# Graph attention over 32 graphs: softmax weights made as [source, target] without turns, scores and sums as extra columns, rows spread through HBM, stages of three graphs interleaved

## The chip, the core and the metric

The kernel runs on one NeuronCore of a Trainium2 chip. The metric is device time in microseconds (us) from the first to the last instruction of one launch. The inputs lie in HBM, 32 graphs of 512 nodes with 512 features each, and everything is computed in float32 except the masks.

## The reference

Each graph goes through a layer norm and a ReLU, then through two graph-attention layers, and the input is added at the end. Cut to what is computed:

```
def gat_layer(x, mask, W, a_src, a_dst, bias, concat):      # H heads of F features
    xl = (x @ W).reshape(B, N, H, F)
    asrc = einsum('bnhf,hf->bnh', xl, a_src)                 # score of a node as source
    adst = einsum('bnhf,hf->bnh', xl, a_dst)                 # score of a node as target
    e = leaky_relu(asrc[:, :, None, :] + adst[:, None, :, :], 0.2)
    e = where(mask[..., None], e, -1e9)
    attn = softmax(e, axis=1)                                # over the sources
    out = einsum('bsdh,bshf->bdhf', attn, xl)
    return (out joined over heads, or their mean) + bias

mask = (adj > 0) | eye
h = relu(layernorm(x))
h = elu(gat_layer(h, mask, W1, as1, ad1, b1, concat=True))   # 4 heads of 256
y = x + gat_layer(h, mask, W2, as2, ad2, b2, concat=False)   # 1 head of 512
```

## The kernel before

All tiles have 128 partitions, and a graph's 512 nodes make four blocks of 128. A framework schedules the program: the code gives the operations and the pools of buffers, and the framework decides the order of each engine's queue and sets the semaphores. So the code's order is only a start, and what stands behind what on an engine has to be read from the built program. Each engine works through its queue in order. All DMAs are issued by SyncE (SP).

The main loop runs over the graphs, b = 0 to 31. `front(b)` normalises x (VectorE), turns it on TensorE to [feature, node] (`pht`, line 139, through an identity matrix), and turns the mask to [target, source] in bf16 (`pm`, line 153). GpSimd adds the second bias to x (line 141).

First layer. `scores` multiplies the four 128-row pieces of the turned input with a narrow matrix `v1` of 8 columns (W applied to the attention vectors; `prow`, line 162), turns the rows back to columns (`pcol`, line 167), and `softmax` spreads one row of scores over all 128 partitions by a product with a selecting matrix of 8 or 2 rows (`bc`, line 178). For each block of targets and each head it then computes the scores on ScalarE (line 185), the leaky ReLU on VectorE (line 186), mask and minimum in one instruction (line 187), and the exponential with its sum on ScalarE (line 191). The product x @ W1 (`pxl`, line 223) has 512 columns to a matmul and is copied out of PSUM by ScalarE (line 227). For each head, VectorE divides the weights by their sums (line 233), `turned` turns them to [source, target] with sixteen transposes on TensorE (`ppt`, line 204) and four copies on VectorE (line 205), and the aggregation (`po`, line 240) gives [feature, target]. Bias and ELU follow on VectorE and ScalarE (lines 247 to 251).

Second layer. The same with one head: narrow scores `prow` with 2 columns, `bc`, softmax, the product with W2 (`pxm`, line 264, copied at line 269), four `ppt` groups, the aggregation (`po`, line 276), then scale, add and store (line 280).

PSUM has eight banks: three for the products (`mm`), two for turns (`tp`), two for the spread rows (`bc`), one for scores. A float32 matmul appears in the profile as two instructions, each with a weight load of its own on PEld; a float32 transpose as one.

Of the kernel before, what the change touches and what calls it, by code (L numbers as in the profile page):

```python
# [8 lines left out]
F32 = mybir.dt.float32  # L9
# [4 lines left out]
PSUM = bass.MemoryType.PSUM  # L14

P = 128
# [12 lines left out]
def tile_gat(  # L29
# [30 lines left out]
    assert N == 512 and D == 512 and DO == D and HF % 512 == 0  # L60
# [3 lines left out]
    psum = ctx.enter_context(tc.tile_pool(name="psum", bufs=1, space=PSUM))  # L64

    X, ADJ = {}, {}

    def load(b):
        X[b] = work.tile([P, NT, D], F32, tag="x", name=f"x{b}")
        nc.sync.dma_start(X[b], x[b].rearrange("(t p) d -> p t d", p=P))  # L70
        for t in range(NT):
            a = work.tile([P, N], I32, tag="adj", name=f"adj{b}_{t}", bufs=4)
            nc.sync.dma_start(a, adj[b, t * P : (t + 1) * P, :])
            ADJ[b, t] = a

    load(0)

# [5 lines left out]
    pick = const.tile([2 * H, H, P], F32, name="pick")  # L83
    nc.vector.tensor_copy(pick, identf[: 2 * H, :H, None].to_broadcast([2 * H, H, P]))
# [3 lines left out]
    w1_sb = const.tile([P, KT, HF], F32, name="w1_sb")  # L88
    nc.sync.dma_start(w1_sb, w1.rearrange("(k p) f -> p k f", p=P))
    w2_sb = const.tile([P, FT, DO], F32, name="w2_sb")  # L90
    nc.sync.dma_start(w2_sb, w2.rearrange("(k p) f -> p k f", p=P))
    b1_sb = const.tile([P, FT], F32, name="b1_sb")
    nc.sync.dma_start(b1_sb, b1.rearrange("(c p) -> p c", p=P))
    b2_sb = const.tile([P, DO], F32, name="b2_sb")
    nc.sync.dma_start(b2_sb, rows_of(b2, P))

    # What gives the scores of a row: W applied to the attention vectors.
    v1 = const.tile([P, KT, 2 * H], F32, name="v1")
    v2 = const.tile([P, FT, 2], F32, name="v2")
    for s, (a1, a2) in enumerate(((as1, as2), (ad1, ad2))):  # L100
        for h in range(H):
            a_bc = work.tile([P, FH], F32, tag="p", name=f"a1_{s}_{h}", bufs=8)
            nc.sync.dma_start(a_bc, rows_of(a1[h], P))
            for k in range(KT):
                junk = work.tile([P, FH], F32, tag="et", name=f"j1_{s}_{h}_{k}", bufs=3)
                nc.vector.scalar_tensor_tensor(
                    junk, w1_sb[:, k, h * FH : (h + 1) * FH], 1.0, a_bc, op0=OP.mult, op1=OP.mult,
                    accum_out=v1[:, k, s * H + h : s * H + h + 1],
                )
        a_bc = work.tile([P, DO], F32, tag="p", name=f"a2_{s}", bufs=8)  # L110
        nc.sync.dma_start(a_bc, rows_of(a2[0], P))
        for k in range(FT):
# [8 lines left out]
    def front(b):  # L121
# [3 lines left out]
        for t in range(NT):  # L125
            nc.vector.bn_stats(stats[:, t, :], X[b][:, t, :])
            nc.vector.bn_aggr(mv[:, t, :], stats[:, t, :])
# [186 lines left out]
```

## Time and profile before

| | |
|---|---|
| runs, us | 4168.31, 4171.07, 4169.6 (median 4169.6) |
| span of the profiled execution, us | 4169.4 |
| what lies around the span, against the median, us | 0.2 |
| TensorE busy | 4119.9 us, 99% |
| VectorE busy | 2195.5 us, 53% |
| ScalarE busy | 1451.3 us, 35% |
| GpSimd busy | 202.7 us, 5% |
| mean granted TensorE clock | 0.987 |
| moved by DMA | 108.85 MB, 26 GB/s on average |

The profile is one execution. Its groups give, for each line, engine and tile, the number of instructions and the mean duration of one; matmul durations there overlap each other, so the pace of a run of matmuls is better read from the chain of waits, which gives start, length and count of a stretch of work in order of time. The windows give the busy time of each engine in a stretch, the granted TensorE clock (PEclk, 1.00 is full), the share of the DMA engines in use and the rate.

### The profile page before, as it was taken

Reading aid. Unit: us, or ns where it says so; the run is one execution under the profiler, and the core shown is the slowest. Engines: PE = TensorE matmul, PEld = TensorE weight load, DVE = VectorE, ACT = ScalarE, POOL = GpSimd, SP = SyncE. Lnnn points to the kernel's source line nnn. Section 1 sums busy time; section 2 is a strip of 40 time slices with the busy share of each in tenths; the row PEclk is TensorE's granted clock in tenths of the full one; section 3 lists DMA queues with packets and bytes.
Section 4 is the critical chain, followed back from the end, with each engine's and each line's share of the span. In section 5 each row is a group of like instructions: output and inputs, shape, how many; then the busy total and the mean of one; then the engine's idle time right before and its main releaser. Section 6 shows DMA issues by size and latency. Waiting matters only on the chain.

```text
span 4169.4 us, 33610 instructions
## 1 busy us (share of the span) xinstructions
PE 4119.9 (99%) x12096; PEld 1829.8 (44%) x12096; DVE 2195.5 (53%) x4899; ACT 1451.3 (35%) x2945; POOL 202.7 (5%) x166
## 2 busy tenths in 40 slices
PE   8999999999999999999999999999999999999999
PEld 3444444444444444444444444444444444444444
DVE  8454655445554555545565455644546545465444
ACT  3333433334332343323333333433334333343332
POOL 1000000000000000000000000000000000000000
PEclk9999999999999999999999999999999999999999
DMA  3000000000000000000000000000000000000000
GB/s 111 31 31 18 23 21 31 31 23 19 21 31 31 31 11 21 31 31 31 11 27 24 31 31 11 31 21 31 31 13 28 21 31 31 16 23 21 21 10 11
DMA packets 58118, 108.85 MB, mean 26 GB/s; under 512 B 5856, under 2 KB 6880, under 8 KB 57952
## 3 DMA queue, kind: packets, MB, share of 16 engines
q1 hardware_dynamic: 57952, 106.72, 7.5%
q8 instruction: 95, 1.56, 0.2%
q14 instruction: 71, 0.58, 0.0%
HBM read 73.14 MB, written 33.55 MB: 26 GB/s over the span
## 4 chain that ended last, share of the span: by engine, by line
PE 88%; DVE 8%; issue 2%; ACT 1%; DMA 0%; SPq 0%; POOL 0%; DVEq 0%; POOLq 0%
PE pxl L223 22%; PE pxm L264 21%; PE po L240 16%; PE po L276 11%; PE prow L162 8%; PE ppt L204 5%; PE bc L178 3%; DVE p L186 2%; DVE pt L205 2%; PE pht L139 1%; DVE p L187 1%; ACT p L191 1%; DVE p L233 1%; DVE h L251 1%; PE pm L153 1%
## 5 line engine op out<-in xcount | busy, mean ns | idle before, releaser
L205 DVE COPY pt<-ppt 128x512 f32<-128x512 f32 x640 | 415.9, 683 | 1005.2 <-PE ppt L204 1005.1
L223 PE MATMUL pxl<-w_sb,ht 128*128 128x512 f32 x2048 | 942.0, 620 | 0.0
L240 PE MATMUL po<-pt,xl 128*128 128x512 f32 x2048 | 908.6, 596 | 0.8 <-DVE pt L205 0.8
L264 PE MATMUL pxm<-w_sb,h 128*128 128x512 f32 x2048 | 899.9, 595 | 0.0
L185 ACT ACTIVATE p<-bc,nad 128x512 f32<-128x512 f32 x640 | 397.0, 692 | 860.9 <-PE bc L178 703.9
L223 PEld LDWEIGHTS pxl<-w_sb,ht 128*128 128x128 f32 x2048 | 399.9, 198 | 539.5 <-issue 533.0
L240 PEld LDWEIGHTS po<-pt,xl 128*128 128x128 f32 x2048 | 379.6, 190 | 485.3 <-issue 450.6
L264 PEld LDWEIGHTS pxm<-w_sb,h 128*128 128x128 f32 x2048 | 381.5, 190 | 469.9 <-issue 469.9
L191 ACT ACTIVATE p<-p,low 128x512 f32<-128x512 f32 x640 | 458.7, 721 | 213.2 <-DVE low L187 213.0
L276 PE MATMUL po<-xm,pt 128*128 128x512 f32 x1024 | 444.9, 592 | 0.0
L186 DVE SCALAR_TENSOR_TENSOR p<-p 128x512 f32<-128x512 f32 x640 | 414.7, 685 | 49.9 <-ACT p L185 49.7
L187 DVE CUSTOM_DVE_ANT_0 p<-p,mask 128x512 f32<-128x512 f32 x640 | 418.4, 683 | 0.0
L204 PEld LDWEIGHTS ppt<-identf,p 128*128 128x128 f32 x2560 | 286.3, 141 | 288.1 <-DVE pt L205 199.9
L204 PE MATMUL ppt<-identf,p 128*128 128x128 f32 x2560 | 361.6, 279 | 9.3 <-DVE pt L205 7.9
L249 ACT ACTIVATE h<-po,b_sb 128x512 f32<-128x512 f32 x256 | 174.6, 682 | 482.1 <-DVE e L247 482.1
L247 DVE TENSOR_SCALAR e<-po,b_sb 128x512 f32<-128x512 f32 x256 | 191.4, 748 | 249.8 <-PE po L240 249.8
L227 ACT ACTIVATE xl<-pxl 128x512 f32<-128x512 f32 x256 | 148.8, 593 | 479.5 <-PE pxl L223 479.5
L276 PEld LDWEIGHTS po<-xm,pt 128*128 128x128 f32 x1024 | 192.0, 190 | 229.1 <-issue 229.1
L162 PE MATMUL prow<-h,v 128*2 128x512 f32 x512 | 261.2, 592 | 19.8 <-DVE h L251 19.3
L280 DVE SCALAR_TENSOR_TENSOR o<-po,inv,x 128x512 f32<-128x512 f32 x128 | 96.1, 751 | 339.6 <-PE po L276 339.6
L269 ACT ACTIVATE xm<-pxm 128x512 f32<-128x512 f32 x128 | 75.8, 592 | 564.0 <-PE pxm L264 564.0
L141 POOL TENSOR_TENSOR x<-x,b_sb 128x512 f32<-128x512 f32 x128 | 169.2, 1332 | 1633.5 <-DVE hn L134 1623.7
(42 smaller groups left out, 1889.1 us busy)
## 6 DMA issues: line engine op xcount, KB each, us to landing
x<-in_x_dram SPq DMA_DIRECT2D x32, 1024.0 KB, 5.3
adj<-in_adj_dram SPq DMA_DIRECT2D x128, 256.0 KB, 3.4
out_dram<-o SPq DMA_DIRECT2D x128, 256.0 KB, 2.0
w_sb<-in_L_gnn_W_dram SPq DMA_DIRECT2D x2, 2048.0 KB, 13.5
a<-in_L_gnn_att_src_dram SPq DMA_DIRECT2D x4, 128.0 KB, 5.3
a<-in_L_gnn_att_dst_dram SPq DMA_DIRECT2D x4, 128.0 KB, 3.9
b_sb<-in_L_gnn_b_dram SPq DMA_DIRECT2D x1, 256.0 KB, 10.8
a<-in_L_gnn_att_src_dram SPq DMA_DIRECT2D x1, 256.0 KB, 5.2
```

Source lines behind the costliest of these rows:

```text
L162: nc.tensor.matmul(ps, v[:, k, :], r, start=(k == 0), stop=(k == len(rhs) - 1))
L185: nc.scalar.activation(p, bc, AF.Identity, bias=nad[:, d, h : h + 1], scale=-1.0)
L186: nc.vector.scalar_tensor_tensor(p, p, SLOPE, p, op0=OP.mult, op1=OP.min)
L187: nc.vector.tensor_tensor_reduce(out=p, in0=p, in1=MASK[b, d], scale=1.0, scalar=BIG, op0=OP.add, op1=OP.min, accum_out=low[:, d : d + 1],)
L191: nc.scalar.activation(p, p, AF.Exp, bias=low[:, d : d + 1], scale=-1.0, accum_out=tot[:, d : d + 1])
L204: nc.tensor.transpose(pp[:, s, :], p[:, s * P : (s + 1) * P], identf)
L205: nc.vector.tensor_copy(pt[:, :, d * P : (d + 1) * P], pp)
L223: nc.tensor.matmul(ps, ht[:, k, t * P : (t + 1) * P], w1_sb[:, k, c * 512 : (c + 1) * 512], start=(k == 0), stop=(k == KT - 1),)
L240: nc.tensor.matmul(ps, xl[s][:, f * P : (f + 1) * P], pt[:, s, :], start=(s == 0), stop=(s == NT - 1),)
L247: nc.vector.tensor_scalar(e, ps, bias, 0.0, op0=OP.add, op1=OP.min)
L264: nc.tensor.matmul(ps, h1[k][:, t * P : (t + 1) * P], w2_sb[:, k, :], start=(k == 0), stop=(k == FT - 1),)
L276: nc.tensor.matmul(ps, pt[:, s, d * P : (d + 1) * P], xl2[s], start=(s == 0), stop=(s == NT - 1))
```

## The change

Almost all of the function is rewritten. What it does:

- W1 and W2 get extra columns, so that the scores come out of the products themselves: each head's 256 columns become 258 in the first layer (source score, target score, 256 features), and W2's 512 become 514, done as two matmuls of 257. The tiles `xl` and `xl2`, now single and constant, have another column of ones, so that the aggregation gives the sum of the weights as a column of its result: 257 columns in the first layer, 256 and 258 in the second. No matmul of the products has 512 columns any more; there are twice as many.
- The weights are made as [source, target] at once. `soft` (a generator) first turns the source scores to rows (`pas`), writes them to a small DRAM tile and reads them back into all 128 partitions (`oas`, `spread`, lines 188 and 192 of the changed kernel); for each head and block of targets VectorE adds the mask and takes the maximum (line 205). From it come two rows for each head, turned (`prr`), written and read back again (`orr`, two buffers). ScalarE then takes two exponentials for each block of sources (lines 227 and 230), VectorE the greater of them and the lesser of that and the mask (lines 234 and 235, 1024 elements each).
- `prow`, `bc`, `ppt`, the copies behind `ppt` and the scaling of the weights are gone. The aggregation of the first layer gives [target, feature]; it is scaled while it is copied out (one half on ScalarE, line 294, one on VectorE, line 295) and then turned with 32 transposes (`pz`, `turn`, line 267).
- The products' PSUM tiles have two banks each and two buffers (`mm`); `tp` has three, `sc` one.
- x is read a second time for the residual (`xr`, line 328), and GpSimd adds the bias to it there.
- The main loop goes in steps i: `project1(i+1)` with `front(i+2)`, `gather2(i-1)` and `project2(i)` with the softmax of graph i+1's first layer, `gather1(i+1)` with the softmax of graph i's second layer. `run(main, per)` advances the side generators by `per` pieces after each piece of the main one.

The diff, cut to its core:

```diff
-FAR = 1e9
-BIG = 3e38
+BIG = 2.0**100
...
+    w1_sb = const.tile([P, KT, H, W], F32, name="w1_sb")
+    w2_sb = const.tile([P, FT, DO + 2], F32, name="w2_sb")
+    xl = const.tile([P, NT, H, W + 1], F32, name="xl")
+    nc.vector.memset(xl[:, :, :, W : W + 1], 1.0)
+    xl2 = const.tile([P, NT, DO + 3], F32, name="xl2")
...
-    def scores(b, layer, rhs, v, n):
-            nc.tensor.matmul(ps, v[:, k, :], r, start=(k == 0), stop=(k == len(rhs) - 1))
...
-    def softmax(b, layer, rows, nad, n, h):
-        nc.tensor.matmul(bc, pick[: 2 * n, h, :], rows, start=True, stop=True)
...
-    def turned(b, layer, h, ps):
-                nc.tensor.transpose(pp[:, s, :], p[:, s * P : (s + 1) * P], identf)
-            nc.vector.tensor_copy(pt[:, :, d * P : (d + 1) * P], pp)
...
+    def soft(b, layer, n, cols, give):
...
+        def spread(v, rows, per, tag, bufs):
+            k = rows * NT
+            ps = psum.tile([k, P], F32, tag="sc", name=f"p{tag}{name}", bufs=1)
+            nc.tensor.transpose(ps, v, identf)
+            sb = work.tile([k, P], F32, tag=f"r{tag}", name=f"r{tag}{name}")
+            nc.vector.tensor_copy(sb, ps)
+            dr = dram.tile([k, P], F32, tag=f"d{tag}", name=f"d{tag}{name}")
+            nc.sync.dma_start(dr, sb)
+            got = []
+            for i in range(0, rows, per):
+                o = work.tile([P, per, N], F32, tag=f"o{tag}", name=f"o{tag}{name}_{i}", bufs=bufs)
+                nc.sync.dma_start(
+                    o.rearrange("p r n -> p (r n)"),
+                    bass.AP(tensor=dr.tensor, offset=dr.offset + i * N, ap=[[0, P], [1, per * N]]),
+                )
+                got.append(o)
+            return got
+
+        asr = spread(sc[:, 0].rearrange("p h t -> p (h t)"), n, n, "as", 1)[0]
+        yield
+        for h in range(n):
+            for d in range(NT):
+                nc.vector.tensor_tensor_reduce(
+                    out=junk, in0=asr[:, h, :], in1=MASKT[b][:, d, :], scale=1.0, scalar=-BIG,
+                    op0=OP.add, op1=OP.max, accum_out=mx[:, h, d : d + 1],
+                )
+                if d % 2:
+                    yield
...
+        rr = spread(r.rearrange("p h i t -> p (h i t)"), 2 * n, 2, "rr", 2)
+        yield
+        for h in range(n):
+            p = work.tile([P, NT, N], F32, tag="p", name=f"p{name}_{h}", bufs=4)
+            for t in range(0, NT, 2):
+                e2 = work.tile([P, 2, N], F32, tag="e2", name=f"e2{name}_{h}_{t}", bufs=2)
+                for j in range(2):
+                    nc.scalar.activation(
+                        p[:, t + j, :], rr[h][:, 0, :], AF.Exp, bias=sc[:, 0, h, t + j : t + j + 1]
+                    )
+                    nc.scalar.activation(
+                        e2[:, j, :], rr[h][:, 1, :], AF.Exp, bias=sa2[:, h, t + j : t + j + 1]
+                    )
+                pp = p[:, t : t + 2, :]
+                nc.vector.tensor_max(pp, pp, e2)
+                nc.vector.tensor_tensor(pp, pp, MASK[b][:, t : t + 2, :], op=OP.min)
+                yield
+            give(h, p)
...
+    def project1(b):
+                ps = psum.tile([P, 2, 512], F32, tag="mm", name=f"pxl{b}_{t}_{hp}", bufs=2)
+                        nc.tensor.matmul(
+                            ps[:, j, :W], ht[:, k, t * P : (t + 1) * P], w1_sb[:, k, hp + j, :],
+                            start=(k == 0), stop=(k == KT - 1),
+                        )
+                nc.scalar.activation(xl[:, t, hp : hp + 2, :W], ps[:, :, :W], AF.Copy)
...
+    def gather1(b):
+                        nc.tensor.matmul(
+                            ps[:, j, : FH + 1], p[:, s, d * P : (d + 1) * P], xl[:, s, h, 2 : W + 1],
+                            start=(s == 0), stop=(s == NT - 1),
+                        )
+                nc.vector.reciprocal(inv, ps[:, :, FH : FH + 1])
+                nc.scalar.activation(z[:, dp, :], ps[:, 0, :FH], AF.Copy, scale=inv[:, 0, :])
+                nc.vector.tensor_scalar_mul(z[:, dp + 1, :], ps[:, 1, :FH], inv[:, 1, :])
...
+    def project2(b):
+                    nc.tensor.matmul(
+                        ps[:, j, : W - 1], h1[:, k, t * P : (t + 1) * P],
+                        w2_sb[:, k, j * (W - 1) : (j + 1) * (W - 1)],
+                        start=(k == 0), stop=(k == FT - 1),
+                    )
+            nc.scalar.activation(
+                xl2[:, t, : DO + 2].rearrange("p (c w) -> p c w", c=2), ps[:, :, : W - 1], AF.Copy
+            )
...
+    def gather2(b):
+            xr = work.tile([P, D], F32, tag="xr", name=f"xr{b}_{d}", bufs=3)
+            nc.sync.dma_start(xr, x[b, d * P : (d + 1) * P, :])
+            nc.gpsimd.tensor_tensor(xr, xr, b2_sb, op=OP.add)
...
+    def run(main, per):
+        for _ in main:
+            for _ in range(per):
+                while side:
+                    try:
+                        next(side[0])
+                        break
+                    except StopIteration:
+                        side.pop(0)
...
+    for i in range(-1, B + 1):
+        if i + 2 < B:
+            load(i + 2)
+        if i + 1 < B:
+            if i + 2 < B:
+                side.append(front(i + 2))
+            run(project1(i + 1), 2)
+            finish()
+            side.append(soft(i + 1, 1, H, cols1, keep1(i + 1)))
+        if i >= 1:
+            run(gather2(i - 1), 2)
+        if 0 <= i < B:
+            run(project2(i), 4)
+            finish()
+            side.append(soft(i, 2, 1, cols2, keep2(i)))
...
+            run(gather1(i + 1), 1)
+        finish()
```

How this moves instructions is read from the order in which the built programs hold them. The numbers in the names are graph, then layer or block, then a running number. On TensorE before, between graph 14's second-layer product (`pxm14_3`) and graph 15's first one (`pxl15_0`), the turns and the narrow products stand:

```order
L264 MATMUL pxm14_3_9518<-w2_sb_87,h114_7_9347 128x512
L204 MATMUL ppt14_2_0_0_9530<-identf_74,p14_2_0_0_9464 128x128 x4
...
L276 MATMUL po214_3_9578<-xm14_3_9527,pt14_2_0_9529 128x512
L162 MATMUL prow15_1_9596<-ht15_9364,v1_93 8x512 x3
L223 MATMUL pxl15_0_0_9663<-w1_sb_85,ht15_9364 128x512
L167 MATMUL pcol15_1_9603<-identf_74,rows15_1_9601 128x8 x4
L178 MATMUL bc15_1_0_9610<-rows15_1_9601,pick_81 128x512
L178 MATMUL bc15_1_1_9636<-rows15_1_9601,pick_81 128x512
L223 MATMUL pxl15_0_0_9663<-w1_sb_85,ht15_9364 128x512 x3
```

They are the scores (`prow`, `pcol`) and the spread rows (`bc`) of the softmax of graph 15, put ahead of the product that hides it. On TensorE now, from the end of graph 15's first product to its first aggregation (`po15_0_0`); x8 and x16 are whole tiles:

```order
L251 MATMUL pxl15_3_2_10203<-w1_sb_77,ht15_9413 128x258 x8
L333 MATMUL po213_0_10216<-xl2_83,p13_2_0_9940 128x256
...
L184 MATMUL pas15_1_10233<-identf_66,sc15_1_10229 16x128
...
L333 MATMUL po213_3_10297<-xl2_83,p13_2_0_9940 128x258
L310 MATMUL pxm14_0_10318<-w2_sb_78,h114_9808 128x257 x16
L310 MATMUL pxm14_1_10375<-w2_sb_78,h114_9808 128x257 x7
L184 MATMUL prr15_1_10346<-identf_66,r15_1_10343 32x128
L310 MATMUL pxm14_1_10375<-w2_sb_78,h114_9808 128x257 x9
L310 MATMUL pxm14_2_10423<-w2_sb_78,h114_9808 128x257 x16
L310 MATMUL pxm14_3_10456<-w2_sb_78,h114_9808 128x257 x16
L288 MATMUL po15_0_0_10476<-xl_81,p15_1_0_10360 128x257 x8
```

The softmax of graph 15 now runs beside graph 13's second aggregation and graph 14's second product, with two single turns (`pas` one tile into `gather2`, `prr` seven sixteenths into the second of the four `pxm` tiles) in TensorE's queue. On ScalarE before, the copies of `pxm` stand together, ahead of the softmax of the next graph:

```order
L269 ACTIVATE xm14_1_9505<-pxm14_1_9496 128x512
L269 ACTIVATE xm14_2_9516<-pxm14_2_9507 128x512
L269 ACTIVATE xm14_3_9527<-pxm14_3_9518 128x512
L185 ACTIVATE p15_1_0_0_9615<-bc15_1_0_9610,nad15_1_9608 128x512
L185 ACTIVATE p15_1_0_1_9620<-bc15_1_0_9610,nad15_1_9608 128x512
```

And now, from the copy of the second `pxm` tile on, with the exponentials of the four heads of graph 15 (`p15_1_0` to `p15_1_3`, eight to a head, all but the first and last of some left out):

```order
L315 ACTIVATE xl2_83<-pxm14_1_10375 128x514
L227 ACTIVATE p15_1_0_10360<-orr15_1_0_10352,sc15_1_10229 128x512
...
L227 ACTIVATE p15_1_1_10393<-orr15_1_2_10354,sc15_1_10229 128x512
...
L230 ACTIVATE e215_1_2_2_10416<-orr15_1_4_10356,sa215_1_10231 128x512
L315 ACTIVATE xl2_83<-pxm14_2_10423 128x514
L227 ACTIVATE p15_1_3_10441<-orr15_1_6_10358,sc15_1_10229 128x512
...
L230 ACTIVATE e215_1_3_2_10449<-orr15_1_6_10358,sa215_1_10231 128x512
L315 ACTIVATE xl2_83<-pxm14_3_10456 128x514
```

The copy of the third `pxm` tile stands behind 24 exponentials, and that of the fourth behind 32. It is so in every graph but the first and the last.

More of the change, by code (lines that the diff above doesn't have):

```diff
@@ L14 @@
 PSUM = bass.MemoryType.PSUM
+DRAM = bass.MemoryType.DRAM
 P = 128
@@ L64, in tile_gat @@
     psum = ctx.enter_context(tc.tile_pool(name="psum", bufs=1, space=PSUM))
[L66 to L76, printed above, removed]
+    dram = ctx.enter_context(tc.tile_pool(name="dram", bufs=2, space=DRAM))
     identf = const.tile([P, P], F32, name="identf")
@@ L271, in tile_gat @@
[L271 to L279 removed]
+            inv = work.tile([P, 1], F32, tag="inv2", name=f"inv2{b}_{d}", bufs=2)
```

307 lines of the change are left out of this document (160 added, 147 removed).

## The prediction

> **What bounds the kernel now.** I read the page first, for shares, then the chain of waits in order of time, for the pace of each stage and the length of a graph's turn, then the windows, for the clock. On the page, these are the span and the busy times:
>
> ```profile
> span 4169.4 us, 33610 instructions
> PE 4119.9 (99%) x12096; PEld 1829.8 (44%) x12096; DVE 2195.5 (53%) x4899; ACT 1451.3 (35%) x2945; POOL 202.7 (5%) x166
> ```
>
> TensorE is never free, and nothing else is near full. From the chain of waits (start us, length us, what), one graph in the middle:
>
> ```profile
> 2056.44 25.95 PE pxm L264 x60
> 2082.39 0.87 PE ppt L204 x8
> 2083.26 0.95 PE prow L162 x2
> ...
> 2098.98 2.67 PE prow L162 x6
> ...
> 2103.05 1.82 PE bc L178 x4
> 2104.87 28.50 PE pxl L223 x62
> ...
> 2234.41 28.50 PE pxl L223 x62
> ```
>
> A graph takes 2234.41 - 2104.87 = 129.5 us; 32 of them are 4145, and some 24 us are start and end. An instruction of 512 columns (half a float32 matmul) paces at 25.95/60 = 0.4325 us, a float32 transpose of 128 columns at 0.87/8 = 0.109, a narrow `prow` or `bc` at 0.45 to 0.48, as much as a full one. `pxl` has the same shape as `pxm`, but takes 28.50 where 62 x 0.4325 = 26.8: 1.7 us go elsewhere. The windows (stretch, length, busy times, then PEclk, DMA share, GB/s) show where:
>
> ```profile
> 2102.00:2105.40 3.40, 3.40 (x12) 1.28 (x11) 1.18 (x4) 1.35 (x3) 0.00 (x0) 1.00 0.81 277
> 2105.40:2108.80 3.40, 3.40 (x6) 1.33 (x5) 3.40 (x9) 3.40 (x8) 0.00 (x0) 0.57 0.00 0
> ```
>
> The clock is halved for some 3.4 us right behind `pcol` and `bc`, matmuls of 8 rows.
>
> **What TensorE loses and gains.** Per graph go 24 `prow` (two instructions for each of 12 matmuls, x 0.46 = 11.0), 10 `bc` (4.7), 80 `ppt` (8.7), `pcol` (0.7) and the halved clock behind them (1.7). In come 32 `pz` and 4 single turns (36 x 0.109 = 3.9). The products' 224 instructions of 512 columns (96.9 us) become 448 of 256 to 258. From the two paces above (0.4325 at 512 columns, 0.109 at 128) a line gives 0.218 at 258; a fixed part of twice the size would give 0.221. I take 0.220: 98.6 us. What is left is `pht` (16 x 0.109) and the bf16 `pm`, 0.61/8 each:
>
> ```profile
> 2052.11 0.61 PE L153 MATMUL pm<-identb,am 128*128 128x128 bf16 x8
> ```
>
> So TensorE has 98.6 + 3.9 + 1.7 + 1.2 = 105.4 us of work per graph, 3373 in all. Without a wait, that would be a fifth off. VectorE and ScalarE are not the bound: per graph VectorE has 2195.5/32 = 69 us, and loses 20 copies (`pt`), 20 leaky ReLUs and 16 scalings while 20 operations of double length come in; ScalarE stays at about 45.
>
> **What now ends last.** The softmax of the next graph has two trips through HBM in it, and TensorE's queue holds its two turns (`pas`, `prr`) in line, so everything behind a late turn waits. I follow it from `pas`, with these rows (page of DMA issues: KB each, us to landing; groups; timelines):
>
> ```profile
> x<-in_x_dram SPq DMA_DIRECT2D x32, 1024.0 KB, 5.3
> adj<-in_adj_dram SPq DMA_DIRECT2D x128, 256.0 KB, 3.4
> out_dram<-o SPq DMA_DIRECT2D x128, 256.0 KB, 2.0
> L171 DVE TENSOR_SCALAR nad<-pcol 128x16 f32<-128x16 f32 x32 | 5.6, 174 | 22.3 <-PE pcol L167 22.3
> L280 DVE SCALAR_TENSOR_TENSOR o<-po,inv,x 128x512 f32<-128x512 f32 x128 | 96.1, 751 | 339.6 <-PE po L276 339.6
> L227 ACT ACTIVATE xl<-pxl 128x512 f32<-128x512 f32 x256 | 148.8, 593 | 479.5 <-PE pxl L223 479.5
> 2008.78 0.68 DVE L187 CUSTOM_DVE_ANT_0 p<-p,mask 128x512 f32<-128x512 f32 x1
> 2009.39 0.08 DVE L187 DVE_READ_ACCUMULATOR2_ANT low<- 128x1 f32 x1
> 2009.39 0.69 DVE L187 CUSTOM_DVE_ANT_0 p<-p,mask 128x512 f32<-128x512 f32 x1
> 2104.05 2.42 ACT L185 ACTIVATE p<-bc,nad 128x512 f32<-128x512 f32 x4 [21.02 <-PE bc L178]
> ```
>
> The mask-and-maximum is the same custom operation as line 187: one every 0.61 us. ScalarE makes one 128x512 every (2.42 - 0.69)/3 = 0.58.
>
> A row spread to all partitions is read 128 times from the same few KB, and the start of the trace shows that this is slower than a plain load. At 28 to 31 us the queue serves one such load of 128 KB and the next one begins; at 33 us it serves plain ones:
>
> ```profile
> 28.00:29.00 1.00, 1.00 (x3) 0.38 (x2) 1.00 (x7) 0.57 (x1) 0.00 (x0) 1.00 0.71 61
> 29.00:30.00 1.00, 1.00 (x4) 0.46 (x3) 1.00 (x7) 0.00 (x0) 0.00 (x0) 1.00 0.98 91
> 33.00:34.00 1.00, 1.00 (x4) 0.49 (x3) 1.00 (x3) 0.00 (x0) 0.00 (x0) 1.00 1.06 401
> ```
>
> 91 GB/s against 401, with the engines as busy. That source is a row of 1 KB; `oas` reads 8 KB and `orr` 4 KB, so I expect less of it. The 1 MB of `oas`: 5.3 us as a plain load, 2.0 + 1.05 MB/91 GB/s = 13.5 at the slow rate; I take 7.0, nearer the plain row, as the source is eight times as wide. The 0.5 MB of `orr`: 4.0 (between the plain rows) to 7.8; I take 4.8.
>
> GpSimd's bias add now falls beside the maxima, as `xr` is loaded behind the stores of the graph before. In the start of the trace VectorE's two-input operation on 256 elements (line 106) takes this with and without GpSimd's add (line 141) beside it:
>
> ```profile
> 21.08 5.50 POOL L141 TENSOR_TENSOR x<-x,b_sb 128x512 f32<-128x512 f32 x4 [9.79 <-DMA b_sb<-in_L_gnn_b_dram]
> 22.56 1.48 DVE L106 SCALAR_TENSOR_TENSOR j<-w_sb,a 128x256 f32<-128x256 f32 x1
> 29.56 0.41 DVE L106 SCALAR_TENSOR_TENSOR j<-w_sb,a 128x256 f32<-128x256 f32 x1
> ```
>
> So an add costs VectorE 1.07 us; three in the stretch, 3.0 (0 to 4.3). This agrees with the Trainium skill, "SBUF — State Buffer", section "Who interferes with whom": a VectorE instruction with two SBUF inputs contends with a GpSimd one that reads SBUF, and the later one waits for the whole of the earlier. By that rule alone, with GpSimd always second, the 3.0 would be 0 and the time 90 us less.
>
> *First wait, at `prr`.* Copy 0.2, write 2.0, issue 0.5, `oas` 7.0, 16 maxima x 0.61 = 9.8, one scaling with its reciprocal among them 0.9, GpSimd 3.0, four small operations 0.7: 24.1 us after `pas`. TensorE has three tiles of `gather2` (3 x 16 x 0.220 = 10.5), one of `project2` (7.05) and 14 instructions of 32 of the next (3.1) in between: 20.6. Wait 3.5 us (none with the plain load and no GpSimd cost; 5.5 with both at 1 us more).
>
> *Second wait, at the first tile of `gather1`.* Its PSUM buffer is that of the third `pxm` tile, whose copy stands behind 24 exponentials on ScalarE. From `prr`: copy 0.3, write 2.0, issue 0.5, `orr` 4.8, 24 x 0.58 = 13.9, the third head's row (its buffer is free only when the first head is done: 0.5 + 4.8 against the 4.6 us of the second head) 0.6, the copy 0.6: 22.7. TensorE's work there is 18 instructions and two tiles: 18.1. Wait 4.6 us (3.2 to 6.5).
>
> *Third wait, at its second tile.* Eight more exponentials, the last row and the copy 5.6, against one tile of 3.5: 2.1 us (1.6 to 2.6).
>
> *Small ones inside `gather1`,* all from the softmax of the second layer: scaling the outputs stands behind a maximum that waits for its row; ScalarE's copy of the last tile behind eight exponentials; the last `pz` behind both. Together 3.5 us (2 to 5), estimated from the same durations.
>
> Waits S = 3.5 + 4.6 + 2.1 + 3.5 = 13.7 us per graph (6.8 to 19.6). Idle may halve the clock again: at the start of the trace, 2.95 us of idle after `bc` did it.
>
> ```profile
> 56.01 2.07 PE L178 MATMUL bc<-rows,pick 8*128 8x512 f32 x2 [2.95 <-ACT p L185]
> 54.00:56.00 2.00, 0.00 (x0) 0.00 (x0) 2.00 (x8) 2.00 (x6) 0.00 (x0) 0.62 0.00 0
> 56.00:58.00 2.00, 1.99 (x2) 0.50 (x2) 2.00 (x5) 1.93 (x5) 0.00 (x0) 0.50 0.00 0
> ```
>
> It costs 1.7 us each time, as in `pxl`, but falls behind the first and second wait, where ScalarE's copy and not TensorE ends the next one: I add nothing (up to 1.7 more, within the range). The Trainium skill, "TensorE: Matmul & The Clock Gate", Part 1, halves the clock after an idle window of about 3.4 us; here 2.95 sufficed, with narrow matmuls ahead of it. By that rule the second wait surely counts: 1.7 x 30 = 51 us more if nothing hid it.
>
> **Start and end.** The first product needs all attention vectors, as the first `prow` does now:
>
> ```profile
> 40.47 3.60 PE L162 MATMUL prow<-ht,v 128*8 128x512 f32 x8 [0.52 <-DVE j L106]
> ```
>
> I take 38 us. Graph 0's softmax has nothing beside it: 0.9 + 0.2 + 2.0 + 0.5 + 7.0 + 9.8 + 0.7 + 7.6 + one head of 4.6 = 34 (rounded up for its last operations). Graph 1's has only `project2(0)`, 28, and its 24 exponentials: 14 of wait. The last second-layer softmax: 24; the last store 3. Together 113.
>
> **The sum.** 3373 + 113 + 30 x 13.7 = 3897 us, of one execution whose before has 4169.4, 0.2 below the median, so it is taken for the median too. With S = 6.8 it is 3690, with 19.6 4074, and 4090 with some halved clock. No change would need S = 22.8.
>
> **Rivals.**
>
> *Spread reads at the slow rate* (slower). If 8 KB and 4 KB sources crawl as the 1 KB one does, `oas` costs 6.5 more, each `orr` 3.0, of which three follow one another in a graph's turn, and the second layer's two loads 4 in all: S = 13.7 + 6.5 + 9 + 4 = 33, time 4480. It decides from 9.1 us per graph, about half of that. For it: the rows at 28 us. Against: the wider source. Chance 0.12.
>
> *Weight loads are not hidden* (about the old time). Each instruction of 258 columns still brings a load:
>
> ```profile
> L264 PEld LDWEIGHTS pxm<-w_sb,h 128*128 128x128 f32 x2048 | 381.5, 190 | 469.9 <-issue 469.9
> L204 PEld LDWEIGHTS ppt<-identf,p 128*128 128x128 f32 x2560 | 286.3, 141 | 288.1 <-DVE pt L205 199.9
> ```
>
> 190 ns of 220. If load and matmul paced at 0.250, 448 x 0.03 = 13.4 us come per graph, some 5 of them inside the waits: 3897 + 32 x 8.5 = 4170. Against it: transposes pace at 0.109 although their loads last 0.141, so loads overlap. Chance 0.05.
>
> *The interleaving hides it all* (faster). S near 5: 3636 (3560 to 3690). It needs plain-load times and no GpSimd cost; against it, the order on ScalarE stands whatever the loads do. Chance 0.11.
>
> **How the numbers follow.** Forecast 0.72, 3690 to 4090, likeliest 3897. A measurement of this kernel can tell about 0.2%, 8 us. Faster: the forecast, the fast rival and half of the weight loads, 0.85; slower: the slow reads and a little of the weight loads, 0.13; same 0.02. The range leaves out the fast rival and the slow ones above 4090.
>
> **What would show it.** Right: `pxl` and `pxm` instructions pacing at 0.218 to 0.221; TensorE waiting at `prr` for VectorE and at `po` of a new graph for ScalarE's copy, not for the weights; `oas` landing at 6 to 8 us, `orr` at 4 to 6; a turn of about 119 us. Wrong: a matmul pace of 0.25; `oas` over 10 us; waits below 5 or above 23 us per graph; VectorE without a gap.

## The result and the profile after

The changed kernel takes 3807.97 us (median of 4 runs, 3800.51 to 3810.58), the kernel before 4169.5 (median of 4, 4168.31 to 4171.07): a ratio of 0.913, with a 95% interval of 0.9117 to 0.9143. Forecast were 3897 us, 3690 to 4090. The profiled execution of the changed kernel took 3810.58 us with a span of 3808.8; the numbers below are of that span.

The page after, span and busy times:

```profile
span 3808.8 us, 42519 instructions
PE 3457.8 (91%) x16512; PEld 2950.1 (77%) x16512; DVE 2212.1 (58%) x4549; ACT 1351.1 (35%) x2305; POOL 223.9 (6%) x166
```

TensorE went from 99% of a longer span to 91% of a shorter one: it has less to do, and now it waits. Its pace, from the chain of waits (start us, length us, what):

```profile
1909.16 3.48 PE po L333 x16
...
2014.31 10.50 PE pxl L251 x48
2024.80 3.48 PE po L333 x16
```

An instruction of 256 to 258 columns takes 3.48/16 = 0.2175 to 10.50/48 = 0.2188 us, and this turn 2024.80 - 1909.16 = 115.64 us. Over all 31 turns, from the first `prr` at 90.38 to the last at 3668.61, the mean is 115.4. Where the turn waits stands in TensorE's timeline (start, length, line, what, and in brackets the idle time before it with what ended it):

```profile
1912.47 0.27 PE L184 MATMUL pas<-identf,sc 128*16 128x128 f32 x1
1912.58 10.61 PE L333 MATMUL po<-xl,p 128*128 128x256 f32 x48
1923.03 10.17 PE L310 MATMUL pxm<-w_sb,h 128*128 128x257 f32 x46
1936.86 0.40 PE L184 MATMUL prr<-identf,r 128*32 128x128 f32 x1 [3.67 <-DVE r L219]
1937.05 20.74 PE L310 MATMUL pxm<-w_sb,h 128*128 128x257 f32 x82
1959.74 3.73 PE L288 MATMUL po<-xl,p 128*128 128x257 f32 x16 [1.95 <-ACT xl L315]
1965.13 2.87 PE L288 MATMUL po<-xl,p 128*128 128x257 f32 x12 [1.65 <-ACT xl L315]
```

These are the three waits that the prediction named, in its places and with its releasers: `prr` for VectorE, `gather1`'s first two tiles for ScalarE's copy. There is a fourth loss that no bracket shows: 82 `pxm` instructions behind `prr` take 20.74 us instead of 82 x 0.219 = 18.0. The windows (stretch, length, busy times, then PEclk, DMA share, GB/s) say why:

```profile
1935.00:1936.00 1.00, 0.00 (x0) 0.00 (x0) 0.97 (x3) 0.00 (x0) 0.00 (x0) 0.89 0.00 0
1936.00:1937.00 1.00, 0.14 (x1) 0.14 (x2) 0.70 (x6) 0.00 (x0) 0.00 (x0) 0.50 0.00 0
...
1942.00:1943.00 1.00, 1.00 (x4) 0.79 (x4) 0.00 (x0) 0.00 (x0) 0.00 (x0) 0.69 1.02 418
```

The wait of 3.67 us halves the clock from 1935.8 to 1942.6 (0.89 and 0.69 are the means of the slices in which it changes), and TensorE loses 2.8 us by it. So this turn has 3.67 + 1.95 + 1.65 us of waits and 2.8 of clock: 10.1. TensorE's work is 104.7 us (measured below, in first_no_bias_add), so another 0.9 us of the 115.64 stands in no bracket.

What `prr` waits for is VectorE's maxima. Their timeline, with the first and the last of GpSimd's four additions to `xr` in the second fence:

```profile
1919.95 0.75 DVE L340 SCALAR_TENSOR_TENSOR xr<-po,inv,xr 128x512 f32<-128x512 f32 x1
1920.62 0.68 DVE L205 CUSTOM_DVE_ANT_0 junk<-oas,mt 128x512 bf16<-128x512 f32 x1
1921.34 1.63 DVE L205 CUSTOM_DVE_ANT_0 junk<-oas,mt 128x512 bf16<-128x512 f32 x1
1923.02 0.69 DVE L205 CUSTOM_DVE_ANT_0 junk<-oas,mt 128x512 bf16<-128x512 f32 x1
1923.75 0.69 DVE L205 CUSTOM_DVE_ANT_0 junk<-oas,mt 128x512 bf16<-128x512 f32 x1
```

```profile
1921.10 1.32 POOL L329 TENSOR_TENSOR xr<-xr,b_sb 128x512 f32<-128x512 f32 x1 [28.31 <-DMA xr<-in_x_dram]
...
1931.68 1.65 POOL L329 TENSOR_TENSOR xr<-xr,b_sb 128x512 f32<-128x512 f32 x1 [4.43 <-DMA xr<-in_x_dram]
```

Two things are to be seen. A maximum that starts during an addition (1921.34, the addition at 1921.10) lasts 1.63 us, another 0.69 (there are three of the long ones and one of 1.09); and a plain one follows the one before after 0.73 us (1923.02 to 1923.75), not after 0.61. Third, ScalarE between `prr` and `gather1`, first and last of its 24 exponentials:

```profile
1943.91 0.60 ACT L315 ACTIVATE xl<-pxm 128x514 f32<-128x514 f32 x1 [13.12 <-PE pxm L310]
1944.41 0.71 ACT L227 ACTIVATE p<-orr,sc 128x512 f32<-128x512 f32 x1
...
1958.50 0.71 ACT L230 ACTIVATE e<-orr,sa 128x512 f32<-128x512 f32 x1
1959.11 0.58 ACT L315 ACTIVATE xl<-pxm 128x514 f32<-128x514 f32 x1
```

The copy of the third `pxm` tile at 1959.11, which frees `gather1`'s first buffer, stands behind all 24. Last, the trips through HBM, from the chain of graph 0, where nothing else is in the way:

```profile
72.01 1.35 DMA das<-ras
73.39 4.50 DMA oas<-das
...
91.11 1.38 DMA drr<-rrr
...
93.27 3.67 DMA orr<-drr
```

### The profile page after: what moved, and what is told of

Same layout as the page of the kernel before. It is cut to its first block, busy times and chain, and to the rows that moved or that the text cites. A ratio compares the mean times of both kernels' runs of the same rounds, so it can differ in the third digit from the quotient of the medians.

```text
span 3808.8 us, 42519 instructions
## 1 busy us (share of the span) xinstructions
PE 3457.8 (91%) x16512; PEld 2950.1 (77%) x16512; DVE 2212.1 (58%) x4549; ACT 1351.1 (35%) x2305; POOL 223.9 (6%) x166
## 4 chain that ended last, share of the span: by engine, by line
PE 63%; DVE 16%; ACT 15%; DMA 4%; issue 2%; SPq 0%; ACTq 0%; POOL 0%; DVEq 0%
PE pxl L251 23%; PE po L288 21%; DVE junk L205 11%; PE po L333 9%; ACT e L230 7%; ACT p L227 7%; PE pxm L310 4%; PE pz L267 3%; DMA orr<-drr 2%; PE pht L150 2%; DVE xr L340 1%; DVE p L235 1%; DMA drr<-rrr 1%; DVE p L234 1%; PE pm L165 1%
## 5 line engine op out<-in xcount | busy, mean ns | idle before, releaser
L288 PE MATMUL po<-xl,p 128*128 128x257 f32 x4096 | 966.0, 391 | 134.2 <-ACT xl L315 109.8
L288 PEld LDWEIGHTS po<-xl,p 128*128 128x128 f32 x4096 | 780.2, 196 | 266.5 <-ACT xl L315 132.8
L310 PE MATMUL pxm<-w_sb,h 128*128 128x257 f32 x4096 | 947.7, 393 | 0.0
L251 PE MATMUL pxl<-w_sb,ht 128*128 128x258 f32 x4096 | 933.4, 382 | 12.6 <-DVE j L101 12.6
L310 PEld LDWEIGHTS pxm<-w_sb,h 128*128 128x128 f32 x4096 | 807.9, 198 | 127.0
L234 DVE TENSOR_TENSOR p<-p,e 128x1024 f32<-128x1024 f32 x320 | 391.7, 1224 | 336.9 <-ACT e L230 336.9
L205 DVE CUSTOM_DVE_ANT_0 junk<-oas,mt 128x512 bf16<-128x512 f32 x640 | 542.5, 848 | 44.3 <-DMA oas<-das 27.3
L227 ACT ACTIVATE p<-orr,sc 128x512 f32<-128x512 f32 x640 | 454.7, 711 | 61.4 <-DMA orr<-drr 60.8
L333 PE MATMUL po<-xl,p 128*128 128x256 f32 (+1 forms) x2048 | 456.7, 381 | 10.3 <-DVE p L235 10.3
L230 ACT ACTIVATE e<-orr,sa 128x512 f32<-128x512 f32 x640 | 454.2, 710 | 0.0
L333 PEld LDWEIGHTS po<-xl,p 128*128 128x128 f32 x2048 | 387.1, 190 | 70.6 <-ACT e L230 10.6
```

The lines of the kernel that those rows point to most:

```text
L205: nc.vector.tensor_tensor_reduce(out=junk, in0=asr[:, h, :], in1=MASKT[b][:, d, :], scale=1.0, scalar=-BIG, op0=OP.add, op1=OP.max, accum_ ...
L227: nc.scalar.activation(p[:, t + j, :], rr[h][:, 0, :], AF.Exp, bias=sc[:, 0, h, t + j : t + j + 1])
L230: nc.scalar.activation(e2[:, j, :], rr[h][:, 1, :], AF.Exp, bias=sa2[:, h, t + j : t + j + 1])
L234: nc.vector.tensor_max(pp, pp, e2)
L251: nc.tensor.matmul(ps[:, j, :W], ht[:, k, t * P : (t + 1) * P], w1_sb[:, k, hp + j, :], start=(k == 0), stop=(k == KT - 1),)
L288: nc.tensor.matmul(ps[:, j, : FH + 1], p[:, s, d * P : (d + 1) * P], xl[:, s, h, 2 : W + 1], start=(s == 0), stop=(s == NT - 1),)
```

## The experiments

My theory was the prediction's: a graph's turn is TensorE's work plus the waits that follow from the places of a few operations in the orders of VectorE and ScalarE. The rivals: TensorE's own halved clock ends the turn; or the HBM trips do; or each operation is as slow as it is and its place doesn't matter. All times are medians beside the kernel before on the same chip (4167 to 4171 us); "mean turn" is from the first layer-one `prr` to the last, 31 turns.

| kernel | us | ratio to before, 95% interval | mean turn, us |
|---|---|---|---|
| changed kernel | 3808.0 | 0.9117 to 0.9143 | 115.4 |
| two_junk | 3739.7 | 0.8954 to 0.8989 | 113.1 |
| no_bias_add | 3716.4 | 0.8899 to 0.8925 | 112.4 |
| copies_first | 3774.5 | 0.9039 to 0.9066 | 114.2 |
| no_interleave | 4099.5 | 0.9821 to 0.9854 | 124.2 |
| copies_and_scalings_first | 3628.9 | 0.8697 to 0.8721 | 109.8 |
| first_no_bias_add | 3477.1 | 0.8336 to 0.8358 | 105.1 |
| all_in | 3480.8 | 0.8344 to 0.8367 | 105.1 |
| split_rows | 3843.8 | 0.9213 to 0.9238 | 116.5 |
| store_twice | 3906.4 | 0.9363 to 0.9388 | 118.5 |

### two_junk: the maxima's single output buffer

```diff
-  junk = work.tile([P, N], BF16, tag="junk", name=f"junk{name}_{h}_{d}", bufs=1)
+  junk = work.tile([P, N], BF16, tag="junk", name=f"junk{name}_{h}_{d}", bufs=2)
```

> The output row that the 16 maxima write (junk, not read by anything) gets two buffers instead of one, so that a maximum need not wait for the one before. Theory (the softmax chain through VectorE and ScalarE sets the turn): a maximum is paced at 0.61 us instead of 0.73, the last one ends 16 x 0.12 = 1.9 us earlier, and everything behind it, the exponentials and the first tile of gather1, comes 1.9 us earlier in each of 31 turns, however TensorE's own idle time and clock are shared out before that: 3808 - 59 = about 3749 us, and the wait at prr shrinks from 3.67 to 1.8 (to 3.1 where prr stands 6 instructions earlier in TensorE's order). Rival A (TensorE's halved clock behind the wait at prr is what ends the turn): with a shorter wait the clock stays full and 2.8 us come on top, 4.7 per graph: 3662. Rival B (the single buffer costs nothing, the pace of 0.73 is the instruction's own): 3808, no change.

Measured: 3739.7, 68 us less. VectorE's and TensorE's timelines:

```profile
1993.18 0.68 DVE L205 CUSTOM_DVE_ANT_0 junk<-oas,mt 128x512 bf16<-128x512 f32 x1
1993.79 0.68 DVE L205 CUSTOM_DVE_ANT_0 junk<-oas,mt 128x512 bf16<-128x512 f32 x1
```

```profile
2001.15 1.98 PE L310 MATMUL pxm<-w_sb,h 128*128 128x257 f32 x8 [1.35 <-DVE xr L340]
2004.84 0.28 PE L184 MATMUL prr<-identf,r 128*32 128x128 f32 x1 [1.71 <-DVE r L219]
2004.96 19.30 PE L310 MATMUL pxm<-w_sb,h 128*128 128x257 f32 x88
2026.39 8.25 PE L288 MATMUL po<-xl,p 128*128 128x257 f32 x28 [2.14 <-ACT xl L315]
```

The pace is 0.61 and the gain close to the theory's 59; rival B is out. 88 instructions in 19.30 us are 0.219 each: two idle stretches of 1.35 and 1.71 us leave the clock whole behind `prr`, yet rival A's 146 did not come. The halved clock has moved: behind `gather1`'s wait of 2.14 us, 28 instructions take 8.25 us instead of 6.1.

### no_bias_add: GpSimd beside the maxima

```diff
-  nc.gpsimd.tensor_tensor(xr, xr, b2_sb, op=OP.add)
```

> GpSimd's addition of the output bias to the residual row is left out (the bias of the second layer is missing from the output). Theory: three maxima of a graph, now 1.63 us long with such an addition beside them and 0.69 without, lose 0.94 us each and a fourth 0.4, so prr comes 3.2 us earlier: the wait at prr falls from 3.67 to about 0.5, and a turn shortens by 2.8 to 3.2 us: 3808 - 31 x 3.0 = 3715 us. Rival A (the halved clock ends the turn): no idle, no halved clock, another 2.8 us: 3628. Rival B (VectorE waits beside GpSimd in any case for something else, as the row from HBM): 3808.

Measured: 3716.4, 92 us less, as the theory had it (93). TensorE's timeline, ScalarE's first exponential, and a window behind the wait at `gather1`:

```profile
1998.82 0.28 PE L184 MATMUL prr<-identf,r 128*32 128x128 f32 x1 [0.43 <-DVE r L219]
1998.95 17.99 PE L310 MATMUL pxm<-w_sb,h 128*128 128x257 f32 x82
2020.29 8.25 PE L288 MATMUL po<-xl,p 128*128 128x257 f32 x28 [3.35 <-ACT xl L315]
```

```profile
2004.94 0.72 ACT L227 ACTIVATE p<-orr,sc 128x512 f32<-128x512 f32 x1 [1.28 <-DMA orr<-drr]
```

```profile
2022.00:2023.00 1.00, 1.00 (x3) 0.72 (x3) 0.55 (x2) 1.00 (x3) 0.00 (x0) 0.50 0.00 0
```

The 2.8 us of halved clock behind `prr` are gone (17.99 instead of 20.74), but the wait at `gather1` is 3.35 instead of 1.95, and the clock is halved behind that one (28 instructions in 8.25 us instead of 6.1): most of what the clock gave is taken back. The clock had also cost something that I had not seen: the first exponential now starts 2004.94 - 1998.82 = 6.1 us behind `prr` and waits for `orr`; before it started 7.55 us behind (1944.41 - 1936.86), directly behind the copy of the second `pxm` tile, which the halved clock had made late.

### copies_first: the copies ahead of the exponentials

```diff
+  with tc.high_priority():
       nc.scalar.activation(
           xl2[:, t, : DO + 2].rearrange("p (c w) -> p c w", c=2), ps[:, :, : W - 1], AF.Copy
       )
```

> ScalarE's copy of the second product's tiles gets precedence over the exponentials in the order: on ScalarE the third tile's copy now stands behind 9 exponentials instead of 24, the fourth behind 18 instead of 32. Theory: the two waits of gather1's first tiles for that copy (1.95 and 1.65 us) go, the 2.8 us of the halved clock in front of them stay and are now the turn's own: 3808 - 31 x 3.6 = 3696 us, the wait at prr unchanged at 3.7. Rival A (the halved clock was not hidden behind the wait but causes it): less than half of that gain, above 3750. Rival B (the exponentials themselves are late, the weights of the first head end the turn and not the copy): a wait of about the same length appears at gather1 for VectorE instead, 3800 or more.

Measured: 3774.5, a gain of 34 instead of 112. My theory missed a wait. The row of TensorE's waits that is new (total us, times, longest), and VectorE's and TensorE's timelines:

```profile
PE po L288 <- DVE z L295: 98.9, 32, 5.0
```

```profile
1950.17 0.48 DVE L295 TENSOR_SCALAR z<-po,inv 128x256 f32<-128x256 f32 x1
```

```profile
1950.70 5.03 PE L288 MATMUL po<-xl,p 128*128 128x257 f32 x22 [3.05 <-DVE z L295]
```

The waits for the copy are all gone. But `gather1` now reaches its third tile while the last exponentials and their maxima are still being made, and the scaling that empties its buffer stands behind those. It is the same fault one step later: rival B's wait in size, on another operation. The time lies where rival A had put it too (above 3750), but the new row alone, 98.9 us, is more than the 78 us of gain that are missing.

### copies_and_scalings_first: the scalings too

On top of copies_first:

```diff
+  with tc.high_priority():
       nc.vector.reciprocal(inv, ps[:, :, FH : FH + 1])
       nc.scalar.activation(z[:, dp, :], ps[:, 0, :FH], AF.Copy, scale=inv[:, 0, :])
       nc.vector.tensor_scalar_mul(z[:, dp + 1, :], ps[:, 1, :FH], inv[:, 1, :])
```

> As copies_first, and the scalings of gather1's outputs (reciprocal, ScalarE's and VectorE's half) get precedence over the exponentials and maxima as well. Theory: the 3.05 us per graph for which TensorE waited at the third tile of gather1 in copies_first (98.9 us in all, for VectorE's scaling behind the last exponentials and their maxima) go, and nothing takes their place, as the weights of the last head are ready some 8 us before TensorE needs them: 3774 - 94 = 3680 us; the wait at prr stays at 3.7. Rival (the exponentials and maxima themselves have no slack, whatever stands between them): TensorE waits for the weights or the second layer's row instead, 3740 or more.

Measured: 3628.9, 146 us below copies_first instead of 94. Of TensorE's waits in each turn only the one at `prr` is left:

```profile
1950.71 0.40 PE L184 MATMUL prr<-identf,r 128*32 128x128 f32 x1 [3.67 <-DVE r L219]
1950.90 19.22 PE L311 MATMUL pxm<-w_sb,h 128*128 128x257 f32 x82
```

The first two turns, where graphs 0 and 1 have little beside their softmax, fell by 9.7 and 13.7 us, which I had not counted. That leaves some 29 us, 0.9 a turn. They fit a halved clock that followed the wait of 3.05 us in some turns of copies_first (see the last section): the mean granted clock rose from 0.9635 to 0.970, by an estimate from these two 58 us less at half clock and 29 less lost. No run takes it out alone.

### first_no_bias_add: does the clock count where nothing hides it?

Both edits together: copies_and_scalings_first without the line of no_bias_add.

> copies_and_scalings_first with GpSimd's addition of the output bias left out (missing from the output). The same omission alone gave 92 us, as the halved clock's loss behind the wait at prr lay inside the waits for ScalarE's copy. Theory (the halved clock is hidden only where such a wait follows): in copies_and_scalings_first no wait follows, so now both go, 3.2 us of wait and 1.2 of clock a graph: 3629 - 31 x 4.4 = 3492 us. Rival (the clock's loss was never in the sum, hidden or not): 3629 - 92 = 3537.

Measured: 3477.1 (3492 forecast), a gain of 152 from the edit that gave 92 on the changed kernel.

```profile
1974.28 0.28 PE L184 MATMUL prr<-identf,r 128*32 128x128 f32 x1 [0.42 <-DVE r L219]
1974.40 17.99 PE L311 MATMUL pxm<-w_sb,h 128*128 128x257 f32 x82
...
2079.38 0.28 PE L184 MATMUL prr<-identf,r 128*32 128x128 f32 x1 [0.43 <-DVE r L219]
```

3.25 us of wait and 19.22 - 17.99 = 1.2 of clock went, and no wait came for them. The turn is 2079.38 - 1974.28 = 105.1 us, 0.4 of it waiting: TensorE's work is 104.7 us per graph, forecast as 105.4.

### all_in: the complete kernel with these waits removed

The two buffers of two_junk and the precedence of copies_and_scalings_first, and the bias moved (`b2_sb` gets a zero column at each end, for the score columns):

```diff
-  nc.scalar.activation(
-      xl2[:, t, : DO + 2].rearrange("p (c w) -> p c w", c=2), ps[:, :, : W - 1], AF.Copy
-  )
+  with tc.high_priority():
+      nc.vector.tensor_tensor(
+          xl2[:, t, : DO + 2].rearrange("p (c w) -> p c w", c=2), ps[:, :, : W - 1],
+          b2_sb.rearrange("p (c w) -> p c w", c=2), op=OP.add,
+      )
...
-  nc.gpsimd.tensor_tensor(xr, xr, b2_sb, op=OP.add)
```

> Nothing is left out. Two buffers for the maxima's junk; the output bias is added by VectorE where the second product's tile is taken out of PSUM (the weights sum to one, so it comes out as the same bias), instead of by GpSimd on the residual row and a copy on ScalarE; that copy and gather1's scalings have precedence. Theory (all waits of a graph are places in VectorE's and ScalarE's orders): prr is ready before TensorE comes to it, no idle, no halved clock, no wait at gather1; what is left is TensorE's 105.4 us a graph, 129 of start and end and some small waits of 0.5 a graph: 3373 + 129 + 15 = 3517 us (3490 to 3560). Rival A (a wait of the same size turns up elsewhere, as in copies_first; VectorE has now 3 us more): 3650 or more. Rival B (the HBM trips of the rows set the turn): the waits at prr or for the first head's weights stay, 3680 or more.

Measured: 3480.8, 36 below the theory's value and 9 below its range (the first two turns again); the rivals are out. It is the best complete version: 0.836 of the time before, 0.914 of the changed kernel's.

### no_interleave: the softmaxes written out at once

```diff
   side.append(soft(i + 1, 1, H, cols1, keep1(i + 1)))
+  finish()
...
   side.append(soft(i, 2, 1, cols2, keep2(i)))
+  finish()
```

> Both softmaxes are written out at once where they can begin, instead of step by step between the tiles of the products. TensorE's order hardly changes by that (the gather2 and project2 matmuls still stand between pas and prr), ScalarE's does: one of the four copies of project2 stands ahead of all 32 exponentials and three behind. Theory (the order on ScalarE, not the amount of work, makes the waits): prr comes 3.5 us earlier as the maxima start one gather2 tile earlier, but the fourth project2 tile must wait for the second's copy behind 32 exponentials: it begins 51.8 us into the turn instead of about 43, with a wait of some 16 us there and gather1 beginning near 59 instead of 50.6; with the last wait of 1.65 gone, 6.8 us more per graph: 4019 us, and up to 4130 if the clock is halved behind so long a wait. Rival (TensorE's own work and the chain to prr set the turn, the interleaving by steps is worth nothing): 3808 or, with prr 3.5 us earlier, 3700.

Measured: 4099.5, in the theory's range. TensorE's timeline:

```profile
1966.48 9.51 PE L310 MATMUL pxm<-w_sb,h 128*128 128x257 f32 x32 [10.97 <-ACT xl L315]
```

The fourth `pxm` tile waits 11.0 us (some 16 forecast) for the copy of the second, behind 32 exponentials, and loses 2.5 more by the clock (9.51 instead of 7.0). Writing the softmaxes out step by step between the products is thus worth 291 us of the 362 that the change gains.

### store_twice: longer trips

```diff
   nc.sync.dma_start(dr, sb)
+  nc.sync.dma_start(dr, sb)
```

> Each row that goes through HBM is stored twice, one store behind the other, before it is spread: a trip is longer by a store (1.4 us) and what the queue puts in between. The first one (das) now stands behind the store of gather2's first tile, and the load of oas behind that of the second, which is scaled 2.9 us later than the load is issued now. Theory (a trip lengthens the chain to prr and to the exponentials, less a slack of about 1 us at each): 2 to 2.6 us later at prr and some 1 us at the exponentials, 31 x 3 = 93 more: 3900 us (3870 to 3930). Rival A (TensorE's products cover the trips): within 15 of 3808. Rival B (every trip's whole delay is on the path, four trips a graph): above 3960.

Measured: 3906.4, 98 us more; both rivals are out. TensorE's timeline:

```profile
1985.70 0.39 PE L184 MATMUL prr<-identf,r 128*32 128x128 f32 x1 [4.46 <-DVE r L220]
2008.85 8.85 PE L289 MATMUL po<-xl,p 128*128 128x257 f32 x28 [5.07 <-ACT xl L316]
```

`prr` comes 27.35 us behind `pas` (at 1958.35) instead of 24.39, more than the theory's 2 to 2.6 later. TensorE has ten more instructions ahead of it in its order (56 of `pxm` instead of 46), so the wait at `prr` itself does not grow: in all 32 turns it is 126.3 us against 141.6. The delay shows at the copy behind the exponentials, 191.2 us in all against 109.8 in the changed kernel.

### split_rows: is the load of `oas` on the path?

```diff
-  asr = spread(sc[:, 0].rearrange("p h t -> p (h t)"), n, n, "as", 1)[0]
+  asr = spread(sc[:, 0].rearrange("p h t -> p (h t)"), n, min(n, 2), "as", 2)
...
-  in0=asr[:, h, :]
+  in0=asr[h // 2][:, h % 2, :]
```

> The first row spread over all partitions (oas, 1 MB) is loaded as two loads of two heads each, so that the first maxima need only the first half. Theory: the load is not on the path, as the maxima stand behind the third gather2 tile's scaling on VectorE, 0.9 us later than the load lands: no change, 3808 within 12 us. Rival (the maxima wait for the load, as the prediction's sum had it with 7.0 us for it): half a load less, 2.2 us in each of 31 turns, 3740.

Measured: 3843.8, 36 us more; neither. The page's DMA issues (KB each, us to landing), then VectorE's timeline:

```profile
oas<-das SPq DMA_DIRECT2D x64, 512.0 KB, 5.2
```

```profile
1934.26 0.69 DVE L205 CUSTOM_DVE_ANT_0 junk<-oas,mt 128x512 bf16<-128x512 f32 x1 [2.34 <-DMA oas<-das]
```

The rival's 68 us of gain did not come, but the test is not clean: the first half lands no sooner than the whole did (5.2 us against 4.50 above; both halves are moved at once), and the order had moved the maxima ahead of a scaling, so that they waited for it. In the turn shown `prr` still comes 24.46 us behind `pas`, as before (24.39); what the turn loses stands behind `gather1`'s first wait, where 28 instructions take 8.25 us, the halved clock again. The mean granted clock is 0.958 against 0.965. By an estimate from these two that is 56 us more at half clock, or 28 us lost where TensorE is busy, most of the 36; the rest stays open.

## Why the prediction held, point by point

The sum was 3373 + 113 + 30 x 13.7 = 3897. In the same terms the runs give 32 x 104.7 = 3350 for TensorE's work (first_no_bias_add), 30 x 10.9 = 327 for the waits and the clock (the mean turn behind the first, 115.6, less 104.7), and so 131 for start and end: 3808.

**TensorE's work** was right: 0.2175 to 0.2188 us an instruction against 0.220, and 104.7 us per graph against 105.4. The rival of weight loads that are not hidden falls by this pace.

**First wait, 3.5 forecast, 3.67 measured,** and the chain from `pas` to `prr` 24.39 us (1912.47 to 1936.86) against 24.1. Two of its terms were wrong and cancelled. Up to the first maximum I took 9.7 us, with 7.0 for `oas`; it was 8.15, and the maximum followed directly on the third tile's scaling, which waits for TensorE; so the load of `oas` was not what it waited for. The maxima I took at 0.61; they went at 0.73, since each waits for the buffer of the one before, and two_junk shows that this alone is worth 68 us. That the two cancelled is luck. GpSimd's cost (3.0) was right: three maxima 0.94 us longer and a fourth 0.4, and no_bias_add gave the 92 us that follow.

**Second wait, 4.6 forecast, 1.95 measured.** The mechanism stood: copy behind 24 exponentials. Two sizes were off. "I add nothing" for the halved clock was wrong by 1.4 us: the clock takes 2.8 us here (1.7 forecast), and it is not only hidden behind the wait, as I argued, but delays the second `pxm` tile's copy, which stands in front of the first exponential. Against that, the trip (`drr` 1.38 for 2.0, `orr` 3.67 for 4.8) was 1.5 us shorter: 6.1 us from `prr` to the first exponential where the clock is whole, against 7.6. So `prr` to `gather1` took 22.9 us against 22.7, and 1.95 of wait with 2.8 of slow clock stand where 4.6 of wait were forecast. One edit's 92 us on the changed kernel and 152 on copies_and_scalings_first fit a clock's loss that is covered in part where a wait follows and counts where none does. They do not measure it alone, as on the changed kernel a halved clock came back behind `gather1`'s wait.

**Third wait, 2.1 forecast, 1.65 measured.** Right.

**Small waits inside `gather1`, 3.5 forecast,** was the step that failed most. In the turn shown no bracket stands behind the second tile. The second layer's maxima and exponentials do stand among `gather1`'s scalings, but the first maximum (1972.69, directly behind a reciprocal) does not wait for its row, and TensorE loses almost nothing by them. In some other turns it waits a little, for the scores of the second layer; the row of TensorE's waits (total us, times, longest) makes that 0.5 us a graph:

```profile
PE pas L184 <- DVE sc L321: 16.5, 13, 1.5
```

The 3.05 us in copies_first are not these waits: there the scalings stand behind the first layer's exponentials and their maxima.

**Start and end, 113 forecast, 131 measured.** Left out was `gather1` of the first two graphs, behind whose tiles exponentials and scalings stand too. Graph 0's ran from 101.53 to 144.70, 43.2 us for 31.6 of work: 6.1 of the difference are waits for scalings, the rest fits a halved clock (32 instructions in 9.50 us, 16 in 6.41). copies_and_scalings_first took 23 us from the first two turns.

**The rivals.** Slow spread reads: `oas` moved 1 MB in 4.50 us, as a plain load does, so it fell; store_twice shows what longer trips cost, 98 us for a second store each. "The interleaving hides it all" was wrong as it stood, and right about what can be had: with the orders mended, S is below 1 and the time 3481. The forecast's 89 us too many are thus 30 x 2.8 = 84 of waits, in which the small ones (3.5 a graph) outweigh the rest; work (23 too many) and start (18 too few) nearly cancel.

## What to carry to other kernels

When a product loses its turns and TensorE begins to wait, look for the small operation that frees its PSUM buffer and for what stands ahead of it in its own engine's order: copies and scalings of PSUM belong ahead of long elementwise runs, all of them at once, as mending one only moves the wait to the next. An output that nobody reads still needs a second buffer, and an addition on GpSimd should not fall beside VectorE's critical run. A halved clock is to be booked at the wait that follows it, and whatever its late tiles release is to be followed as well; when one wait is mended it can come back behind the next, as in two_junk and no_bias_add.

## What was not expected of the hardware

In these traces each change of the granted clock comes a multiple of 3.41 us after the one before. The half clock lasts one such window in the turn of copies_and_scalings_first (1949.97 to 1953.38) and two in the changed kernel's turn above (1935.8 to 1942.6). How long TensorE idles does not decide alone whether it comes. In another turn of the changed kernel a wait of 1.95 us was enough (TensorE's timeline, then two windows):

```profile
1727.50 8.25 PE L288 MATMUL po<-xl,p 128*128 128x257 f32 x28 [1.95 <-ACT xl L315]
1724.16:1727.58 3.42, 1.47 (x8) 0.96 (x6) 3.38 (x4) 3.42 (x7) 0.00 (x0) 1.00 0.18 62
1727.58:1730.99 3.41, 3.41 (x8) 2.73 (x9) 2.93 (x3) 3.41 (x6) 0.00 (x0) 0.50 0.00 0
```

In copies_first the wait of 3.05 us that ends at 1950.70 left the clock whole:

```profile
1945.54:1948.95 3.41, 2.11 (x10) 1.52 (x8) 3.41 (x5) 3.41 (x7) 0.00 (x0) 1.00 0.14 52
1948.95:1952.37 3.42, 1.67 (x8) 1.49 (x9) 3.42 (x6) 0.62 (x2) 0.00 (x0) 1.00 0.07 26
```

The first wait lies within one window, in which TensorE is busy for 1.47 of 3.42 us. The second is cut by the boundary of two, and TensorE is busy for 2.11 and 1.67 us of them. Of another wait of 3.05 us there, which ends at 920.18, 2.05 us fall into one window (918.13 to 921.54, 1.36 us busy), and the clock is halved behind it. So the place of a wait against the windows counts as well as its length, and a turn may lose 1.7 us more or less by it. The Trainium skill, "TensorE: Matmul & The Clock Gate", Part 1, tells of a free-running window of 3.4 us; these traces agree with that length, but the window need not be idle as a whole: 0.43 of it was busy at 1727.58. Nor is busy time the whole measure: in the kernel before the clock was halved behind matmuls of 8 rows, with TensorE busy throughout (the prediction's window from 2102.00 to 2105.40).

A store of 8 or 16 KB that is read back landed in 1.35 and 1.38 us. A 1 MB load whose source is 8 KB, read 128 times, went as fast as a plain one (4.50 us against 5.3), while the 1 KB source of the kernel before went at 91 GB/s.
